# Five small loads moved behind GpSimd's first sums, and two small VectorE instructions moved later, in a two-layer graph attention kernel

## The chip, the cores and the metric

The kernel runs on one core of a Trainium2 chip. The metric is device microseconds (us) of one execution; of the kernel before there are three timed runs, and lower is better. The engines are TensorE (PE, with its weight loads as PEld), VectorE (DVE), ScalarE (ACT), GpSimd (POOL) and SyncE (SP). SP, ACT and POOL issue DMAs. All of them move their bytes on the same 16 DMA engines, through one queue for each issuer: q1 is SP's, q10 is ACT's, and q0, called software_dynamic, is GpSimd's.

## The reference

`x` is 128 graphs of 128 nodes with 512 features, float32; `adj` is one 128x128 matrix of zeros and ones that all graphs share. Two layers follow one another:

```python
# layer 0: masked attention of 8 heads, residual, layer norm
q, k, v = x @ Wq + bq, x @ Wk + bk, x @ Wv + bv
scores  = q k^T / sqrt(64) + (1 - adj) * -1e9
x = layernorm(x + softmax(scores) v @ Wo + bo)
# layer 1: additive attention, residual, layer norm
h  = x @ W
e  = leaky_relu(s1[:, :, None] + s2[:, None, :], 0.2) * adj   # s1 = h a1, s2 = h a2
x = layernorm(x + elu(softmax(e) @ h + beta * h))
```

The inputs that the change touches are `adj`, `beta` (one number), `bo` (512 numbers) and `a` (a1 and a2, 512 numbers each).

## The kernel before

**Tiling.** The 128 graphs are worked off in 64 groups of two (`G = 2`, `NG = 64`). Each big product is done with seven half-size products instead of eight (Strassen's scheme): `weight_sum` makes sums of blocks of a weight, `block_sum` makes differences of blocks of the turned x on GpSimd (n = 1, 2, 3, 4 for the tiles t1 to t4), `product` multiplies, and `take_part` and `add_block` collect the results. For the group g, `load_blocks` fetches x in blocks (tile `xblk`, one buffer, four DMAs), and `turn_x` turns it on VectorE (tile `xT`), once for each of the two graphs.

**Order.** Everything after the setup is written out by hand. `at(place, fn, ...)` puts a call on a list with a place on one common scale; the list is sorted and called in that order, which fixes the order of instructions on every engine and in every issuing queue. Groups lie `STEP = 36.678` apart, and `other` holds the places of single groups. A place is no time: an instruction runs when its engine comes to it and what it needs is there.

```python
    with tc.manual_schedule():
        for _, _, fn, args in sorted(pieces, key=lambda p: p[:2]):
            fn(*args)
```

**What lies around the change,** by engine and in the order of the places:

- SP: `load_blocks(0)` (two of its four DMAs), Wq, then Wk and Wv (`load_k_and_v`), x of graph 0 and of graph 1, `load_blocks(1)`, W (`w_sb`, place 16.793), Wo (19.493), then x and blocks of the next group.
- POOL: the setup's memsets and the identity matrix, the DMA of `adj` (L151), the four DMAs of `load_later` at 0.583 (`beta`, the two halves of `a`, `bo`; each is broadcast to all 128 partitions, L104), then `block_sum` of group 0 in the order n = 3 (7.943), 1 (11.603), 2 (12.383), 4 (16.043), `residual(0)` and `residual(1)` (L435, which add `bo` to x), the sums of Wv (L223 to L229), and `block_sum` of group 1.
- DVE: `turn_x` of group 0, the sums of Wq, `make_beta` at 12.183 (L171: identity times `beta`), the sums of Wk, `make_mask` at 16.043 (L165: (adj - 1) times 1e9), `turn_x` of group 1 (18.983 and 20.013), two `add_block` (21.043 and 21.403), then `wa_column(0, 0)` and `(0, 1)` (L180, 21.883 and 22.613, which read W and the first half of `a`), `add_block("k", 0, 4, 1, 0)` (23.343), `wa_column(0, 3)`, and the first `mask` (L387, 25.353), which reads what `make_mask` made.
- PE: `keep_busy`, 15 products of the identity with itself, the turning of the biases (L140), then the products of group 0, with the first one of group 1 (`product("k", 1, 1)`) at 21.21, and `scores(0)` (L379) at 23.903.

`beta_i`, which `make_beta` makes, is first read by `weights`, well into layer 1 of the first group. `adj_sb` itself is first read again by `edge` (L594), at 80.1 us in the trace.

Of the kernel before, what the change touches and what calls it, by code (L numbers as in the profile page):

```python
# [22 lines left out]
def gnn_two_layers(  # L23
# [34 lines left out]
    nc = tc.nc  # L58
    B, N, D = x.shape
# [10 lines left out]
    cpool = ctx.enter_context(tc.tile_pool(name="const", bufs=1))  # L70
# [31 lines left out]
    def broadcast(pool, src, n, name):  # L102
        t = pool.tile([P, n], F32, tag=name, name=f"{name}_in")
        nc.gpsimd.dma_start(out=t, in_=src.rearrange("(o n) -> o n", o=1).broadcast_to([P, n]))  # L104
        return t
# [5 lines left out]
    for i, src in enumerate((bq, bk, bv)):  # L111
        nc.scalar.dma_start(
            out=bias_rows[i * NC : (i + 1) * NC], in_=src.rearrange("(c p) -> c p", p=P)
# [34 lines left out]
    for t in s2_in:  # L148
        nc.gpsimd.memset(t, 0.0)
    adj_sb = cpool.tile([P, N], F32, tag="adj_sb", name="adj_sb")  # L150
    nc.gpsimd.dma_start(out=adj_sb, in_=adj)  # L151
    later = {}

    def load_later():
        later["beta"] = broadcast(cpool, beta, 1, "beta_b")
        for j in range(2):
            a_j = a1[j * D : (j + 1) * D].rearrange("f o -> (f o)")
            later["a", j] = broadcast(wk2, a_j, D, "uf")
        later["bo"] = broadcast(cpool, bo, D, "bo_b")


    amask = cpool.tile([P, N], F32, tag="amask", name="amask")
# [575 lines left out]
    def at(place, fn, *args):  # L738
        pieces.append((place, len(pieces), fn, args))
# [353 lines left out]
    def lay(g):  # L1093
        own = rows(g) if g < NG - 2 else last_rows(g)
        places = other.get(g, [r[0] for r in own])
        for place, (_, fn, *args) in zip(places, own):
            at(g * STEP + place, fn, *args)

    for g in range(NG):
        lay(g)  # L1100
    at(0.583, load_later)
    at(5.685, load_k_and_v)
    at(8.723, weight_sum, "q", 3, nc.vector)
    at(9.443, weight_sum, "q", 1, nc.vector)
    at(10.163, weight_sum, "q", 2, nc.vector)
    at(10.883, weight_sum, "q", 4, nc.vector)
    at(12.183, make_beta)
    at(13.163, weight_sum, "k", 3, nc.vector)
    at(13.883, weight_sum, "k", 1, nc.vector)
    at(14.603, weight_sum, "k", 2, nc.vector)  # L1110
    at(15.323, weight_sum, "k", 4, nc.vector)
    at(16.043, make_mask)
    at(16.793, load_weight, w1_sb, w1)
    at(19.323, weight_sum, "v", 3, nc.gpsimd)
    at(19.493, load_weight, wo_sb, wo)
    at(20.603, weight_sum, "v", 1, nc.gpsimd)
    at(21.883, wa_column, 0, 0)
    at(22.613, wa_column, 0, 1)
    at(23.343, weight_sum, "v", 2, nc.gpsimd)
# [55 lines left out]
```

## Time and profile before

| | us |
|---|---|
| median of 3 runs | 2377.61 |
| lowest and highest run | 2377.54, 2379.04 |
| the profiled execution: its own time | 2378.15 |
| its span (first to last instruction) | 2376.4 |
| PE busy in the span | 2354.4 (99%) |
| DVE busy | 1961.7 (83%) |
| ACT busy | 1591.1 (67%) |
| POOL busy | 865.5 (36%) |

The span is what the trace covers; 1.75 us lie around it. Times of single instructions are counted from the span's start. A line of a timeline gives start and duration in us, the engine, the line of the code, the operation, the tiles written and read, their shape, the count, and in brackets how long the engine had been idle and what ended that. The share of a DMA queue is the time of its packets over that of all 16 engines in the stretch asked for; it can go over 100% where packets overlap.

### The profile page before, as it was taken

Reading aid. Unit: us, or ns where it says so; the run is one execution under the profiler, and the core shown is the slowest. Engines: PE = TensorE matmul, PEld = TensorE weight load, DVE = VectorE, ACT = ScalarE, POOL = GpSimd, SP = SyncE. Lnnn points to the kernel's source line nnn. Section 1 sums busy time; section 2 is a strip of 40 time slices with the busy share of each in tenths; the row PEclk is TensorE's granted clock in tenths of the full one; section 3 lists DMA queues with packets and bytes.
Section 4 is the critical chain, followed back from the end, with each engine's and each line's share of the span. In section 5 each row is a group of like instructions: output and inputs, shape, how many; then the busy total and the mean of one; then the engine's idle time right before and its main releaser. Section 6 shows DMA issues by size and latency. Waiting matters only on the chain.

```text
span 2376.4 us, 50868 instructions
## 1 busy us (share of the span) xinstructions
PE 2354.4 (99%) x17703; PEld 2177.5 (92%) x17703; DVE 1961.7 (83%) x4390; ACT 1591.1 (67%) x5763; POOL 865.5 (36%) x1044
## 2 busy tenths in 40 slices
PE   8999999999999999999999999999999999999998
PEld 8998999999999999999999999999999999999996
DVE  7788788888888888888888888888888888888887
ACT  4675666766766667667666676676666766766665
POOL 6243333433433333334334333343343333433422
PEclk9999999999999999999999999999999999999999
DMA  6333334334343343343443433424434334344432
GB/s 192 108 100 112 116 101 125 107 105 134 92 120 119 107 118 108 108 128 92 121 122 103 119 108 111 126 92 121 123 103 119 107 112 125 92 120 122 116 115 74
DMA packets 256121, 269.83 MB, mean 114 GB/s; under 512 B 57372, under 2 KB 204840, under 8 KB 255480
## 3 DMA queue, kind: packets, MB, share of 16 engines
q1 hardware_dynamic: 254992, 265.45, 37.8%
q8 instruction: 140, 2.29, 0.4%
q14 instruction: 117, 0.96, 0.1%
q0 software_dynamic: 304, 0.85, 0.1%
q10 hardware_dynamic: 568, 0.27, 0.0%
HBM read 157.62 MB, written 108.85 MB: 112 GB/s over the span
## 4 chain that ended last, share of the span: by engine, by line
PE 96%; DMA 1%; DVE 1%; ACT 1%; issue 0%; SPq 0%; POOLq 0%; POOL 0%; DVEq 0%; ACTq 0%
PE pq L307 12%; PE pk L307 12%; PE pv L301 12%; PE ph L301 11%; PE pw L301 11%; PE eq L307 9%; PE psc L379 5%; PE po L454 5%; PE pz L642 5%; PE eh L301 5%; PE ew L301 4%; PE ev L301 4%; DMA xblk<-in_x_dram 1%; DMA wq_sb<-in_L_gnn_Wq_dram 0%; ACT s L401 0%
## 5 line engine op out<-in xcount | busy, mean ns | idle before, releaser
L435 POOL TENSOR_TENSOR x<-x,bo_b_in 128x512 f32<-128x512 f32 x128 | 163.6, 1279 | 863.3 <-DMA x<-in_x_dram 863.3
L401 ACT ACTIVATE s<-s,nmax 128x128 f32<-128x128 f32 x1024 | 396.9, 396 | 61.4 <-DVE nmax L395 61.3
L415 ACT ACTIVATE sb<-s,rinv 128x128 f32<-128x128 f32 x1024 | 325.3, 392 | 0.0
L355 ACT ACTIVATE kT<-pk,bias_c 128x128 f32<-128x128 f32 x512 | 160.2, 364 | 202.2 <-PE pk L307 143.2
L355 ACT ACTIVATE qT<-pq,bias_c 128x128 f32<-128x128 f32 x512 | 160.6, 368 | 157.6 <-PE pq L307 157.6
L505 DVE SCALAR_TENSOR_TENSOR ya<-w,wa_row 128x512 f32<-128x512 f32 x256 | 223.9, 875 | 4.4
L401 ACT ACTIVATION_READ_ACCUMULATOR s<-s,nmax 128x1 f32 x1024 | 199.2, 195 | 0.0
L466 ACT ACTIVATE oT<-po,bias_c 128x128 f32<-128x128 f32 x512 | 139.5, 382 | 80.5 <-PE po L454 80.5
L352 DVE TENSOR_TENSOR w<-pw,x 128x256 f32<-128x256 f32 x252 | 106.3, 422 | 97.3 <-PE pw L301 90.8
L444 DVE STREAM_TRANSPOSE attnT<-ab 128x512 f32<-128x512 f32 x256 | 172.7, 694 | 6.8 <-DMA ab<-scr 6.6
L387 DVE SCALAR_TENSOR_TENSOR s<-psc,amask 128x512 f32<-128x512 f32 x256 | 168.6, 680 | 0.7 <-PE psc L379 0.7
L395 DVE TENSOR_REDUCE nmax<-s 128x8 f32<-128x1024 f32 x128 | 156.1, 1220 | 4.3
L349 ACT COPY h<-ph 128x256 f32<-128x256 f32 x252 | 93.8, 372 | 94.1 <-PE ph L301 94.0
L349 ACT COPY v<-pv 128x256 f32<-128x256 f32 x256 | 94.6, 369 | 84.4 <-PE pv L301 59.9
L240 DVE STREAM_TRANSPOSE xT<-xblk 128x512 f32<-128x512 f32 x128 | 139.4, 1108 | 7.9 <-DMA xblk<-in_x_dram 7.9
L657 DVE SCALAR_TENSOR_TENSOR u<-h,x 128x512 f32<-128x512 f32 x126 | 87.1, 692 | 63.8 <-ACT h L349 61.6
L260 POOL TENSOR_TENSOR tx<-xT 128x256 f32<-128x256 f32 x128 | 94.7, 741 | 119.8 <-PE psc L379 97.1
L301 PE MATMUL pv<-wv_sb,xT 128*128 128x256 f32 x512 | 137.5, 392 | 0.0
L307 PE MATMUL pq<-xT,wq_sb 128*128 128x128 f32 x1024 | 135.9, 276 | 1.2 <-DMA wq_sb<-in_L_gnn_Wq_dram 1.2
L307 PE MATMUL pk<-xT,wk_sb 128*128 128x128 f32 x1024 | 134.8, 275 | 0.6 <-DMA wk_sb<-in_L_gnn_Wk_dram 0.4
L307 PEld LDWEIGHTS pq<-xT,wq_sb 128*128 128x128 f32 x1024 | 130.1, 193 | 4.5 <-issue 1.3
L307 PEld LDWEIGHTS pk<-xT,wk_sb 128*128 128x128 f32 x1024 | 129.1, 192 | 4.2 <-DMA wk_sb<-in_L_gnn_Wk_dram 0.6
(677 smaller groups left out, 6352.6 us busy)
## 6 DMA issues: line engine op xcount, KB each, us to landing
scr<-sb SPq DMA_DIRECT2D x128, 512.0 KB
ab<-scr SPq DMA_DIRECT2D x512, 128.0 KB
x<-in_x_dram SPq DMA_DIRECT2D x128, 256.0 KB
xblk<-in_x_dram SPq DMA_DIRECT2D x254, 128.0 KB
out_dram<-u SPq DMA_DIRECT2D x126, 256.0 KB
pb<-s2d SPq DMA_DIRECT2D x62, 128.0 KB
attd<-att SPq DMA_DIRECT2D x62, 128.0 KB
ab<-attd SPq DMA_DIRECT2D x248, 32.0 KB
```

Source lines behind the costliest of these rows:

```text
L301: nc.tensor.matmul(out, b[:, c, :], a[:, c, :], start=first and c == 0, stop=(c == 1), skip_group_check=True,)
L307: nc.tensor.matmul(out[:, m * N : (m + 1) * N], a[:, c, m * P : (m + 1) * P], b[:, c, :], start=first and m == 0 and c == 0, stop=(c == 1) ...
L349: nc.scalar.copy(dst, src)
L355: nc.scalar.activation(dst[:, m, :], src[:, m * N : (m + 1) * N], AF.Identity, bias=BIAS[name][:, 2 * i + m : 2 * i + m + 1],)
L387: nc.vector.scalar_tensor_tensor(s_t[b][:, j * HP : (j + 1) * HP, :], psc[b][j], SCALE, amask.rearrange("p (o n) -> p o n", o=1).broadcast ...
L395: nc.vector.tensor_reduce(nmax[b], s_t[b], AX.X, ALU.max, negate=True)
L401: nc.scalar.activation(s_t[b][:, h, :], s_t[b][:, h, :], AF.Exp, bias=nmax[b][:, h : h + 1], accum_out=rsum[b][:, h : h + 1],)
L415: nc.scalar.mul(sb[b][:, :, h, :], s_t[b][:, h, :].rearrange("p (b c) -> p b c", c=Q), rinv[b][:, h : h + 1],)
L435: nc.gpsimd.tensor_tensor(xr[b], xr[b], later["bo"], ALU.add)
L444: nc.vector.transpose(attnT[b].rearrange("p h (a r) -> p a h r", r=Q)[:, rows], ab[b].rearrange("p a (h c) -> p a h c", c=Q)[:, rows],)
L466: nc.scalar.activation(oT[b][:, c, :], src[:, c, :], AF.Identity, bias=bv_c[:, c : c + 1])
L505: nc.vector.scalar_tensor_tensor(z, y[b], 1.0, wa_row[j], ALU.mult, ALU.mult, accum_out=s12[g][:, i, j : j + 1])
```

## The change

The DMA of `adj` leaves the setup and becomes the first of `load_later`. `load_later` now issues `adj`, `beta`, `bo` and the two halves of `a`, in this order; before, `a` came ahead of `bo`. It moves from the place 0.583 to 12.183, which on POOL lies behind `block_sum` n = 3 and n = 1 of group 0 and ahead of n = 2. `make_beta` moves from 12.183 to 21.873 and `make_mask` from 16.043 to 21.878, which on DVE is behind `turn_x` of group 1 and the two `add_block` after it, and right ahead of `wa_column(0, 0)`. No instruction is added or removed.

```diff
-    nc.gpsimd.dma_start(out=adj_sb, in_=adj)
     later = {}
 
     def load_later():
+        nc.gpsimd.dma_start(out=adj_sb, in_=adj)
         later["beta"] = broadcast(cpool, beta, 1, "beta_b")
+        later["bo"] = broadcast(cpool, bo, D, "bo_b")
         for j in range(2):
             a_j = a1[j * D : (j + 1) * D].rearrange("f o -> (f o)")
             later["a", j] = broadcast(wk2, a_j, D, "uf")
-        later["bo"] = broadcast(cpool, bo, D, "bo_b")
...
-    at(0.583, load_later)
     at(5.685, load_k_and_v)
...
-    at(12.183, make_beta)
+    at(12.183, load_later)
...
-    at(16.043, make_mask)
...
+    at(21.873, make_beta)
+    at(21.878, make_mask)
     at(21.883, wa_column, 0, 0)
```

## Prediction

> **What bounds the kernel now.** I read the page's busy times and its chain of waits first, then the chain in order of time for the first 80 us, then the timeline of the engines there, and last the DMA queues in short windows.
>
> From the page, the PE row and the chain by engine:
>
> ```profile
> PE 2354.4 (99%) x17703; PEld 2177.5 (92%) x17703; DVE 1961.7 (83%) x4390; ACT 1591.1 (67%) x5763; POOL 865.5 (36%) x1044
> ...
> PE 96%; DMA 1%; DVE 1%; ACT 1%; issue 0%; SPq 0%; POOLq 0%; POOL 0%; DVEq 0%; ACTq 0%
> ```
>
> TensorE bounds it: only 2376.4 - 2354.4 = 22 us of the span are without a matmul. All that the change touches runs in the first 30 us, once. So it can move the end only by what it adds to or takes from PE's idle time at the start; afterwards PE is full and carries a shift to the end.
>
> The chain of the start, in order of time (start, duration, what):
>
> ```profile
> 1.66 8.48 DMA wq_sb<-in_L_gnn_Wq_dram
> 10.14 0.02 issue
> 10.16 0.33 SPq L81
> 10.49 0.04 issue
> 10.53 0.46 SPq L81
> 10.99 0.04 issue
> 11.04 12.89 DMA xblk<-in_x_dram
> ...
> 25.09 1.08 DVE xT L240
> 26.17 0.30 DVE kT L365
> 26.47 0.34 DVE qT L365
> 26.81 0.04 issue
> 26.86 1.16 PE eq L307 x8
> ```
>
> The start is a DMA chain. Wq lands at 10.14; SP's third and fourth issue of the next group's blocks follow it; the last block lands at 23.93; VectorE turns the blocks until 26.17, adds two results, and only then does PE's product at 26.86 go. PE waited 0.28 us at 25.21 for the turned x and 0.48 us at 26.86. **The landing of xblk of group 1 is what counts,** not the earlier landings by themselves.
>
> What stands right behind that on VectorE, and what waits for it, from the timelines of DVE and of PE's weight loads:
>
> ```profile
> 26.72 1.30 DVE L180 SCALAR_TENSOR_TENSOR wa_t<-w_sb,uf_in 128x512 f32<-128x512 f32 x1
> 28.06 1.09 DVE L180 SCALAR_TENSOR_TENSOR wa_t<-w_sb,uf_in 128x512 f32<-128x512 f32 x1
> 29.08 0.41 DVE L365 TENSOR_TENSOR kT<-eq,kT 128x256 f32<-128x256 f32 x1
> 29.55 1.42 PEld L379 LDWEIGHTS psc<-kT,qT 64*128 64x128 f32 x24 [0.19 <-DVE kT L365]
> ```
>
> VectorE has no gap from 24.05 to 30.3, and PE's scores wait 0.19 us for its add at 29.08. There is no slack between the two.
>
> The two instructions that move, in the same timeline:
>
> ```profile
> 15.21 0.28 DVE L171 TENSOR_SCALAR beta_i<-ident,beta_b_in 128x128 f32<-128x128 f32 x1
> 18.18 0.22 DVE L165 TENSOR_SCALAR amask<-adj_sb 128x128 f32<-128x128 f32 x1
> ```
>
> Now they lie beside idle time of VectorE: it idles 1.56 us ahead of 19.96.
>
> The queues from 8 to 10 us (packets, MB, share of 16 engines):
>
> ```profile
> q0 software_dynamic: 172, 0.57, 76.9%
> q1 hardware_dynamic: 34, 0.19, 23.1%
> ```
>
> GpSimd's loads hold the DMA engines just while the tail of Wq is due.
>
> **What the Trainium skill says.** "SBUF — State Buffer", section "Who interferes with whom": a VectorE `tensor_scalar` can enter a mode with two ports, and one with two SBUF inputs uses the second read port; each then contends with GpSimd, and the later one blocks until the other is through. The trace agrees: the L180 instruction takes 0.68 to 0.69 us with GpSimd idle (from 39.85 on) but 1.30 and 1.09 us beside its sums at 26.20 and 27.43; the 128x512 `tensor_scalar` of L200 takes 0.49 us at 38.79 and 0.98 us at 45.31, beside a sum. "DMA: Bandwidth & Descriptors", section "Anatomy of one DMA — SWDGE (gpsimd) path": about 2.0 us fixed plus bytes/436e3, so an estimate of 2.6 us for 256 KB. Here it is far more: adj (64 KB) landed 4.6 us after its issue, beta 6.1, the two halves of a 7.7 and 8.7, bo 10.8; I use these. The same page, section "Queues, rings and completion order": each engine takes turns between the queues it has work for. The 77 to 23 above is then no fair fight, but a sign that on most engines Wk's packets were not ready before Wq was done (Wk was issued at 6.45).
>
> **The change, part by part.** 1. *Setup on POOL.* adj's issue of 0.71 us at 1.37 goes, so the identity is ready 0.71 us earlier and `keep_busy` ends near 7.4 instead of 8.1. Worth 0: the bias turn waits for the bias DMA until 8.84 and the first real product for Wq. PE idles a little longer before it, and its clock, 0.50 from 11 to 13 us, stays as low: 0.
>
> 2. *Wq.* From 7 to 8 us q1 moved 0.24 MB; 0.19 MB was left for the time after 8. At 0.24 MB/us without q0 this is 0.8 us, so the packets end near 8.8 instead of about 9.6 (landing 10.14 less half a microsecond of receipt, my reading). PE's first product, SP's two issues behind it, and Wk start 0.8 us sooner.
>
> 3. *GpSimd's traffic comes back later.* Its share was 9.8% of 0 to 5, 34.0% of 5 to 10 and 11.7% of 10 to 15 us: 0.49 + 1.70 + 0.59 = 2.8 us of all 16 engines. After the change its issues follow the sum that ends at 8.92: adj 0.71, beta 0.57, then three of 0.55, through 11.85. With the old latencies they land from 13.5 to about 22, in a stretch where q1 alone already fills 90% (10 to 16) and 110% (16 to 24) of the engines, ahead of the xblk landing. So of the 0.77 x 2 = 1.5 us that q0 used from 8 to 10, 0.8 is won by Wk starting sooner and 0.7 is DMA time that now stands empty and is missing later. **xblk lands 0.7 us later.** Bounds: 1.8 us earlier, if the big loads slip behind xblk (0.8, and the 9.8% of 10 to 16 us, 0.6, with some 0.4 of earlier share); 2.8 later, if all the traffic returns with no win. Wk lands earlier (15.0 now), and PE gets through group 0 sooner, but this ends in a longer wait at 25.21: 0.
>
> 4. *POOL's own queue.* 2.93 us of issues stand ahead of `block_sum` n = 2 and 4, which end at 13.5 instead of 10.5. Their first reader is the product at 16.90: even 1.5 us sooner it has them. Behind stands `residual(0)`, which waited for x until 19.68 and now also needs bo, issued at 10.2: 21.0 with 10.8 us. That would hold POOL 1.3 us. Its sums of Wv and of group 1 have slack: t2, ended at 29.74, is read at 33.78, so 4.0 us. Worth 0 up to a bo landing of 23.7.
>
> 5. *SP's queue.* No issue of SP moves in order. Its W load waits for Wk (the waits view), but stands behind the fourth xblk issue, held until 14.55. 0 by itself.
>
> 6. *Beta and mask on DVE.* What leaves 15.21 and 18.18 was in idle time or ahead of sums that PE reads later: 0 gained. At the new place 0.28 + 0.22 = 0.5 us are put between the adds and `wa_column(0, 0)`; queued behind are two of these, the add at 29.08, PE's scores, and then the first mask and the row maximum. All of it shifts, and PE with it. GpSimd is in its sums there, so a wait for the port comes on top: nothing, if it only takes over the 0.6 us that the 1.30 us instruction already pays, up to twice a sum of 1.27 us less that, 1.9. I take 0.1: **0.6 us**, bounds 0.4 and 2.4.
>
> 7. *a for `wa_column`.* a's first half is issued at 10.75 and lands by 18.5 to 21.6 (7.7 to 10.8); needed at 27.2 plus the shift. 0.
>
> Sum: 0.7 + 0.6 = +1.3 us on 2378.15 for the profiled execution, 2379.45; that one stood 0.54 above the median, so 2378.9 as a median.
>
> **The rivals.** *A: the big loads slip behind xblk.* For it: round-robin, and five loads served one after another. Against it: they are on the way from 11 us on. xblk 1.8 earlier, DVE 0.6: -1.2, so 2376.4. *B, slower: the first `wa_column` waits for a.* a is now fourth in q0 and shares the engines with the 512 B pieces of xblk. From a landing at 28.0 on, each microsecond is one of VectorE, and through the add at 29.08 one of PE. Twice the 8.7 us gives 28.2, hardly anything; to cost more than 0.2% it must land near 31.5, 21 us after its issue. Then 2378.9 + 4 = 2383 or more. For it: a latency here grew from 4.6 to 10.8 us within five loads. Against it: the engines never took 20 us. *C: only VectorE's part counts,* since overlapping packets absorb q0: +0.6, 2378.2. That the change is without effect on the order is excluded: the order is by hand.
>
> **How the numbers follow.** The main case and C, which join, have 0.64; A 0.20; B 0.16, of which 0.12 over the bound. 0.2% of 2377.6 is 4.75 us, about what a measurement can tell from no change. No case gains that much: 0.02, out of A's, for what I don't see. Slower by more: 0.12. Within: 0.86. The range goes from A's 2376.2 to 2382.0, the upper bounds of parts 3 and 6 together not quite added; some 0.12 lies above and 0.06 below.
>
> **What would show it.** Right: POOL's five issues between 8.9 and 12; Wq landing near 9.3; Wk before 14.5; q0's share from 8 to 10 near 0; `turn_x` of group 1 at 24.7; beta and mask at 27.4 and 27.7, ahead of L180; a longer PE wait than 0.28 us ahead of `product("k", 1, 1)`; PE's scores 1 to 2 us later. Wrong: `turn_x` before 23.5 (A); DVE idle at L180 with the DMA of a as releaser (B); GpSimd idle for bo past 24; or a difference that arises after 50 us, which nothing here accounts for.

## The result, and the profile after

The changed kernel took **2381.16 us** in the median of 22 runs (2378.8 to 2384.34), the kernel before 2377.63 (2376.19 to 2379.73, 22 runs). The ratio, an estimate from all runs, is 1.0013, with a 95% interval of 1.0007 to 1.0018. The medians lie 3.5 us apart, where 1.3 us were forecast with a range up to 2382.0. This lies within 0.2%, the bound used for the chances, but it is clear of zero, and the forecast lies below the interval (1.7 to 4.3 us).

The profiled execution of the changed kernel took 2379.32 us, 1.8 below the median of its kernel, with a span of 2377.6, only 1.2 us above the profiled span of before. This matters below. The trace shows where 1.2 us come from; it can't show the rest.

The page after: the PE row, and the chain by engine.

```profile
PE 2353.6 (99%) x17703; PEld 2176.6 (92%) x17703; DVE 1962.0 (83%) x4390; ACT 1591.7 (67%) x5763; POOL 866.3 (36%) x1044
...
PE 94%; DMA 2%; DVE 2%; ACT 1%; SPq 1%; issue 0%; POOLq 0%; POOL 0%; ACTq 0%; DVEq 0%
```

PE does the same work. The chain has left PE for DMA and VectorE for a longer stretch, and that stretch is the start. The chain in order of time (start, duration, what):

```profile
10.21 13.89 DMA xblk<-in_x_dram
...
25.25 1.06 DVE xT L240
26.30 0.31 DVE kT L365
26.61 0.04 DVE qT L365
26.65 0.21 issue
26.86 0.50 DVE beta_i L171
27.36 0.69 DVE amask L165
28.05 0.62 DVE wa_t L180 x2
28.69 1.10 DVE wa_t L180 x2
29.79 0.34 DVE kT L365
30.13 1.34 DVE wa_t L180 x2
31.47 1.21 DVE s L387 x2
```

Three things are to be seen. The last block lands at 24.1, as late as before (23.93), although SP issued it 0.8 us sooner. The two instructions that moved, `beta_i` and `amask`, are now links of the chain, 0.50 and 0.69 us long. And PE does not appear in it before 48.56: before, its product at 26.86 was the next link.

The timeline of the changed kernel around PE's wait, with PE and then DVE:

```profile
8.67 1.13 PE L307 MATMUL pq<-xT,wq_sb 128*128 128x128 f32 x8
25.37 2.08 PE L307 MATMUL pk<-xT,wk_sb 128*128 128x128 f32 x8 [3.81 <-DVE xT L240]
27.25 1.56 PE L307 MATMUL eq<-tx,wk_sb 128*128 128x128 f32 x8
...
26.86 0.50 DVE L171 TENSOR_SCALAR beta_i<-ident,beta_b_in 128x128 f32<-128x128 f32 x1
27.28 0.77 DVE L165 TENSOR_SCALAR amask<-adj_sb 128x128 f32<-128x128 f32 x1
27.97 0.68 DVE L180 SCALAR_TENSOR_TENSOR wa_t<-w_sb,uf_in 128x512 f32<-128x512 f32 x1
```

PE starts 1.6 us sooner (8.67 against 10.28) and, in this trace, at full clock. It gets through group 0 and then waits 3.81 us, where it had waited 0.28. After this wait eight matmuls take 2.08 us instead of 1.16: the clock has fallen. The windows of the changed kernel say so (busy us of PE, PEld, DVE, ACT, POOL; then PE's clock, the share of the DMA engines, GB/s):

```profile
24.00:25.00 1.00, 0.00 (x0) 0.00 (x0) 0.77 (x1) 0.00 (x0) 0.92 (x2) 0.94 1.06 391
25.00:26.00 1.00, 0.63 (x3) 0.63 (x4) 1.00 (x2) 0.00 (x0) 0.93 (x1) 0.50 1.05 385
26.00:27.00 1.00, 1.00 (x6) 1.00 (x6) 1.00 (x4) 0.00 (x0) 0.99 (x1) 0.50 1.04 381
```

The first exponential of the first softmax starts at 33.96, against 32.88 before: 1.08 us late. At 60 us the lag is 0.9, and at the end 1.2. In between it wanders, from 0.3 to 2.0 us if one takes every row maximum after 60 us, but it doesn't grow. So all that this trace holds is settled in the first 34 us.

The queues, changed kernel, 8 to 10 us and then 10 to 15 us (packets, MB, share of 16 engines):

```profile
q1 hardware_dynamic: 79, 0.63, 79.8%
```

```profile
q1 hardware_dynamic: 278, 1.53, 76.0%
q0 software_dynamic: 52, 0.08, 5.9%
```

GpSimd's traffic has left the first stretch, as it should. But SP's queue does not take the freed time: from 10 to 15 us it moved 1.53 MB, where before it moved 1.86 MB beside 0.17 MB of GpSimd's. The engines stood partly empty, while SP's issue for W was held from 11.80 for 4.12 us. The last of the experiments comes back to this.

### The profile page after: what moved, and what is told of

It is laid out like the page before. It is cut to its first block, busy times and chain, and to the rows that moved or that the text cites. A ratio compares the mean times of both kernels' runs of the same rounds, so it can differ in the third digit from the quotient of the medians.

```text
span 2377.6 us, 50868 instructions
## 1 busy us (share of the span) xinstructions
PE 2353.6 (99%) x17703; PEld 2176.6 (92%) x17703; DVE 1962.0 (83%) x4390; ACT 1591.7 (67%) x5763; POOL 866.3 (36%) x1044
## 4 chain that ended last, share of the span: by engine, by line
PE 94%; DMA 2%; DVE 2%; ACT 1%; SPq 1%; issue 0%; POOLq 0%; POOL 0%; ACTq 0%; DVEq 0%
PE pq L307 11%; PE pv L301 11%; PE pk L307 11%; PE ph L301 11%; PE pw L301 11%; PE eq L307 9%; PE psc L379 5%; PE po L454 5%; PE pz L642 5%; PE ew L301 4%; PE eh L301 4%; PE ev L301 4%; DMA xblk<-in_x_dram 1%; ACT s L401 0%; ACT sb L415 0%
## 5 line engine op out<-in xcount | busy, mean ns | idle before, releaser
L349 ACT COPY v<-pv 128x256 f32<-128x256 f32 x256 | 94.6, 369 | 84.0 <-PE pv L301 59.6
L260 POOL TENSOR_TENSOR tx<-xT 128x256 f32<-128x256 f32 x128 | 94.6, 740 | 126.1 <-PE psc L379 98.6
```

The source lines that it names most:

```text
L349: nc.scalar.copy(dst, src)
```

## The experiments

All ratios are against the runs of the kernel before on the same chip, with 95% intervals. "Turned at" is the start of `turn_x` of group 1. It comes right after the blocks land, except in `blocks_before`, `blocks_after` and `loads_behind`, where VectorE came to it late and did not wait for them. "Lag" is that of the first exponential behind the profiled execution of before (32.88 us). Both are from one profiled execution of each kernel, while the ratio is from all runs.

| kernel | ratio | interval | turned at | lag | profiled / median us |
|---|---|---|---|---|---|
| before | | | 24.05 | 0 | 2378.15 / 2377.63 |
| changed | 1.0013 | 1.0007 to 1.0018 | 24.23 | 1.08 | 2379.32 / 2381.16 |
| after_again | 1.0013 | 1.0007 to 1.0020 | 23.24 | 0.50 | 2379.07 / 2381.72 |
| late_dve | 1.0001 | 0.9993 to 1.0009 | 24.01 | 1.55 | 2380.00 / 2378.21 |
| late_big | 1.0002 | 0.9993 to 1.0010 | 24.67 | 1.65 | 2379.48 / 2378.72 |
| after_free | 1.0012 | 1.0005 to 1.0018 | 24.12 | 0.87 | 2379.47 / 2381.40 |
| adj_early | 1.0008 | 1.0002 to 1.0015 | 26.39 | 3.42 | 2381.48 / 2380.46 |
| beta_early | 1.0010 | 1.0002 to 1.0018 | 24.61 | 2.23 | 2379.28 / 2380.37 |
| ident_late | 1.0011 | 1.0004 to 1.0018 | 25.06 | 2.07 | 2380.63 / 2380.72 |
| after_warm | 1.0024 | 1.0014 to 1.0034 | 26.95 | 4.48 | 2383.75 / 2383.75 |
| no_big | 1.0001 | 0.9993 to 1.0010 | 20.37 | -2.47 | 2375.96 / 2379.34 |
| blocks_before | 1.0007 | 0.9999 to 1.0016 | 24.93 | 1.93 | 2381.76 / 2380.72 |
| blocks_after | 1.0004 | 0.9996 to 1.0012 | 21.22 | -3.11 | 2377.61 / 2379.43 |
| loads_behind | 1.0016 | 1.0009 to 1.0022 | 24.08 | 0.59 | 2380.71 / 2382.15 |

### The changed kernel again

> The changed kernel once more, unaltered: its first profile ended 1.2 us after that of before, while its median lay 3.5 us above, so another execution is wanted. Theory S (all is settled by the landing of the blocks of group 1, by VectorE's two late instructions and by the clock that PE loses in its longer wait, within the first 50 us): the lag of this execution behind the kernel before at 50 us equals its lag at the end within 0.5 us, and the blocks land later than 24.1 us if the run is longer than 2379.3. Theory L (something later in the span): the lag at 50 us stays near 0.9 us and the rest arises after it. Time 2380 to 2383.

The ratio came back, and the profiled execution (2379.07) was the lowest of its kernel's 21 runs. It shows the same parts in other sizes: the blocks landed 1 us sooner than in the first, the clock fell later, and the end is only 0.9 us behind.

```profile
24.39 1.16 PE L307 MATMUL pk<-xT,wk_sb 128*128 128x128 f32 x8 [1.15 <-DVE xT L240]
25.88 0.28 DVE L171 TENSOR_SCALAR beta_i<-ident,beta_b_in 128x128 f32<-128x128 f32 x1
26.02 1.95 PE L307 MATMUL eq<-tx,wk_sb 128*128 128x128 f32 x8 [0.48 <-DVE qT L365]
26.86 1.11 DVE L180 SCALAR_TENSOR_TENSOR wa_t<-w_sb,uf_in 128x512 f32<-128x512 f32 x1 [0.56 <-DMA w_sb<-in_L_gnn_W_dram]
30.81 1.29 DVE L387 SCALAR_TENSOR_TENSOR s<-psc,amask 128x512 f32<-128x512 f32 x2 [0.55 <-PE psc L379]
```

Here VectorE waited 0.56 us for W, and its first mask 0.55 us for PE, which was at half clock. Blocks that land sooner are not a gain in full: W and the clock come next. What lies between this execution and the median of its kernel, 2.7 us, is not in it, so the two theories stay undecided for that part; for what it holds, the lag of 0.4 us at 51 us and 0.9 at the end agree within 0.5.

### VectorE's two instructions alone

```diff
-    at(12.183, make_beta)
-    at(16.043, make_mask)
+    at(21.873, make_beta)
+    at(21.878, make_mask)
```

> The kernel before with make_beta and make_mask alone moved to 21.873 and 21.878; the loads stay early. Theory S with the VectorE part as the main term: +1.1 us (0.50 + 0.77 us were these two beside GpSimd in the changed kernel, against 0.5 us without it), less the 0.2 us by which they had delayed the sums of Wk, so +0.5 to +1.3. The prediction's own term: +0.6. Rival theory (the loads cost, VectorE's part is hidden): 0 within the interval.

The trace shows a larger price than expected, the runs none. In the profiled execution both instructions took far longer than before, beside GpSimd's sums of Wv at 26.50 and of x at 27.72:

```profile
26.69 1.15 DVE L171 TENSOR_SCALAR beta_i<-ident,beta_b_in 128x128 f32<-128x128 f32 x1
27.77 0.76 DVE L165 TENSOR_SCALAR amask<-adj_sb 128x128 f32<-128x128 f32 x1
30.66 1.61 PE L379 MATMUL psc<-kT,qT 64*128 64x128 f32 x24 [1.14 <-DVE kT L365]
```

1.15 + 0.76 us instead of 0.28 + 0.22, and PE's scores wait 1.14 us for the add behind them. But over the runs the ratio is 1.0001; this execution (2380.0) was next to the slowest of 13 (2377.14 to 2380.03). So VectorE's part, though it is plainly in the chain, is too small to be told from nothing: up to 0.0009, 2.1 us.

### The big loads alone

```diff
-    at(0.583, load_later)
+    at(0.583, load_beta)
...
+    at(12.184, load_later)
```

`load_later` holds only bo and a here, and adj stays in the setup.

> The kernel before with only bo and a (768 KB of the 832 KB) moved behind the first sums; adj and beta stay early, and make_beta and make_mask stay at 12.183 and 16.043. Theory S: Wq lands sooner than 10.14 (near 9.0), the blocks of group 1 near 24 us as in the other two, PE waits over 3 us ahead of its product at 25.2 and runs at half clock after it: about +1.0 us from the clock, or +2.5 if the landing is often later than in the one profile. Rival (VectorE's part is the whole cost): 0 within the interval. Rival of a gain (earlier Wq moves everything): 1 us or more faster.

Wq's first product starts at 9.80, the blocks are turned at 24.67, and PE waits 2.2 us. The clock is at half from 26.8 on. The lag of 1.65 us fits the first theory, but again the runs differ by nothing that can be told: 1.0002. A gain of 1 us is not excluded (0.9993 is 1.7 us); a loss as large as that of the changed kernel is (1.0010 is 2.4 us).

### The changed kernel with beta and mask out of the chain

```diff
+    at(18.973, make_beta)
+    at(18.978, make_mask)
...
-    at(21.873, make_beta)
-    at(21.878, make_mask)
```

> The changed kernel with make_beta and make_mask ahead of turn_x of group 1 (18.973 and 18.978), where VectorE stood idle for 5.6 us; adj and beta have landed by then (14.4 and 15.9 us). Theory S: 1.1 us faster than the changed kernel, because the two instructions leave the chain, so +2.4 on the median of before if the whole median shift of 3.5 is real. Rival (VectorE's part is hidden anyway): as slow as the changed kernel.

The chain of this trace has neither instruction in it, yet the time stays: 1.0012 against 1.0013, where 1.1 us would be 0.0005. The intervals are too wide to exclude the full 1.1 us. But even the lower bound of this kernel, 1.0005, leaves 1.2 us of loss without VectorE's part.

### Which early piece is missed

Three kernels put one piece back. `adj_early` issues adj in the setup again. `beta_early` issues beta at 0.583. `ident_late` leaves all loads late and delays the identity:

```diff
+    pad = cpool.tile([P, 768], F32, tag="pad", name="pad")
+    nc.gpsimd.memset(pad, 0.0)
     make_identity(nc, ident)
```

> The changed kernel with the DMA of adj back in the setup; beta, bo and a stay late, and make_beta and make_mask stay at 21.873 and 21.878. The moved loads bo and a alone came out 0.5 us above the kernel before, make_beta and make_mask alone 0.0, the whole change 3.5. Theory I (the identity is ready 0.7 us sooner, PE warms up too early and then stands idle): the identity is late again here, so near the kernel before, +0 to +1 us. Theory F (GpSimd's very first DMA is dear when nothing small goes ahead of the loads that are waited for): also +0 to +1 us. Theory T (all five loads together late are too many for the stretch): beta is 0.5 KB, so the 64 KB of adj would have to be it, and a third or less is won back.

> The changed kernel with the DMA of beta alone (0.5 KB) issued in the setup's place; adj, bo and a stay late. Theory F: near the kernel before, +0 to +1 us, since a DMA of GpSimd has gone ahead. Theory I: the identity is late again by this issue of 0.57 us, so it too expects a gain; together with the next kernel the two part. Theory T: as slow as the changed kernel, +3 to +3.5.

> The changed kernel with one memset of 128x768 on GpSimd ahead of the identity (about 0.7 us), so that PE's warm-up starts as late as before (2.5 us); all five loads stay late. Theory I: near the kernel before, +0 to +1 us. Theories F and T: as slow as the changed kernel, +3 to +3.5.

All three came out between 1.0008 and 1.0011, below the changed kernel and above the expectation of theories I and F (up to 1 us, 1.0004); the intervals of all three reach down to 1.0004 or below it, and overlap that of the changed kernel. So none of the three pieces is seen to carry the loss alone, and none is cleared either. In two of the traces the blocks land late, and these are worth a look. In `adj_early`:

```profile
22.50 1.06 PE L307 MATMUL pk<-xT,s_k 128*128 128x128 f32 x8
26.39 2.09 DVE L240 STREAM_TRANSPOSE xT<-xblk 128x512 f32<-128x512 f32 x2 [5.75 <-DMA xblk<-in_x_dram]
27.54 1.16 PE L307 MATMUL pk<-xT,wk_sb 128*128 128x128 f32 x8 [3.98 <-DVE xT L240]
29.18 2.08 PE L307 MATMUL eq<-tx,wk_sb 128*128 128x128 f32 x8 [0.48 <-DVE qT L365]
33.71 1.29 DVE L387 SCALAR_TENSOR_TENSOR s<-psc,amask 128x512 f32<-128x512 f32 x2 [0.30 <-PE psc L379]
```

The blocks land 2.3 us later than before, PE waits 3.98 us and then runs at half clock, and the first exponential is 3.42 us late; the span ends 3.3 us late. In the trace's packets the pieces of 512 B, which are the blocks, thin out over three microseconds: 82 of them start from 22 to 23 us, then 62, 38 and 3, while 112 to 145 packets of 2 KB, the next loads, go in each of these microseconds. It looks as if a few of the 16 engines were still at the blocks when the others had gone on; the trace does not name the engine of a packet. **The landing is that of the last piece.**

### Keeping PE's clock up

```diff
+    at(21.2, keep_busy, 11, "warm")
```

> The changed kernel with 11 products of the identity with itself (22 matmul records) on PE at place 21.2, ahead of its wait for the turned blocks of group 1. Theory C (the longer wait lets PE's clock fall to a half, and the next 3 us cost 1 to 2 us more): 1 to 2 us faster than the changed kernel, PE's clock 1.0 from 24 to 29 us. Rival (the clock's fall is hidden by VectorE, which is the slower of the two from 26 to 31 us): no faster; more than 0.5 us slower if the added products end after the blocks land.

It settles nothing on the clock. The added products ran from 23.31 to 25.9, but in this execution the blocks landed at 26.9; PE idled 2.17 us more, and the clock was at half from 29.3 to 32.7. The lag also grows later on, from 5.1 us at 51 us to 6.4 at 269. The added PSUM tile shifts the turn of the eight buffers, which may be why; this is not shown. The ratio is 1.0024.

### Without the big loads

```diff
-        later["bo"] = broadcast(cpool, bo, D, "bo_b")
+        later["bo"] = cpool.tile([P, D], F32, tag="bo_b", name="bo_b_in")
+        nc.gpsimd.memset(later["bo"], 0.0)
...
```

The two tiles of a are filled in the same way, with 0.01.

> The changed kernel with the three big loads of GpSimd (bo and the two halves of a, 768 KB) left out: memsets of the same tiles stand in their place on GpSimd, so bo counts as 0 and a as constant. adj and beta stay late, and nothing else moves. Theory Q (GpSimd's big loads, brought into the stretch in which x and the blocks of group 1 come, make the blocks land late and unevenly): the blocks land at 22.5 us or earlier, PE waits under 2.5 us for them, and the time is 3 to 5 us below the changed kernel, below the kernel before by 0 to 1.5. Rival (the blocks are late by SP's own queue, whose issues run ahead sooner): the blocks at 24 to 26 us as in the changed kernel, and its time within 1 us.

Without the 768 KB the ratio is 1.0001 against 1.0013; the intervals overlap from 1.0007 to 1.0010. Its trace is what was expected:

```profile
20.37 2.13 DVE L241 STREAM_TRANSPOSE xT<-xblk 128x512 f32<-128x512 f32 x2 [1.87 <-DMA xblk<-in_x_dram]
23.05 1.22 DVE L172 TENSOR_SCALAR beta_i<-ident,beta_b_in 128x128 f32<-128x128 f32 x1
27.09 1.61 PE L380 MATMUL psc<-kT,qT 64*128 64x128 f32 x24 [1.20 <-DVE kT L366]
```

The blocks are turned 3.7 us sooner than before, and the next wait is VectorE's part. But only three of its 13 runs (2375.59, 2375.96, 2376.16) are as fast as this; the others lie from 2378.2 to 2381.31. So most executions lose 2 us or more somewhere even without the big loads. That they lose it in the start is likely, but there is no trace of one.

### The blocks ahead in SP's queue

```diff
         load_turned(wk_sb, wk)
+    def load_v():
+        fetch_blocks(1)
         load_turned(wv_sb, wv)
+        fetch_x(0)
```

`load_v` stands at 6.723. `blocks_before` has this on the kernel before, `blocks_after` on `after_free`, with three `wa_column` moved as well. x of graph 0 is at 6.483 in the order and stays ahead of the blocks.

> The kernel before with SP's loads in another order: the blocks of group 1 go ahead of Wv and of x of graph 1 (1.25 MB), instead of behind them; all else as before. If the landing of these blocks is the end of the start's chain, they now land near 19 to 21 us, PE's product for group 1 no longer waits for them, and the gain is what PE waited there, 0.3 and 0.5 us, so 0.5 to 1 us faster. If Wk's landing or VectorE decide instead: 0. If Wv is now late for PE at 31 us: slower by what it waits.

> The changed kernel with make_beta and make_mask ahead of turn_x of group 1, with the blocks of group 1 ahead of Wv and x of graph 1 in SP's queue, and with the first three wa_column behind the first row maxima on VectorE (26.7, 26.8 and 29.0), since W lands no sooner. If the late landing of the blocks is what costs the change its time, the early landing of Wk (11.6 to 13.5 us against 15.1) now reaches PE: blocks at 18 to 21 us, no wait of PE over 1 us after 12 us, 1 to 3 us faster than the kernel before, 4 to 6 below the changed kernel. If a late landing of W or of Wv takes its place: between the two.

On the kernel before it didn't help. Wk, which lies ahead of the blocks, landed later:

```profile
16.63 3.53 PE L311 MATMUL pk<-xT,wk_sb 128*128 128x128 f32 x16 [2.72 <-DMA wk_sb<-in_L_gnn_Wk_dram]
24.93 2.13 DVE L244 STREAM_TRANSPOSE xT<-xblk 128x512 f32<-128x512 f32 x2
```

PE waited 2.72 us for Wk, at half clock after it, and VectorE turned the blocks without any wait for them, behind PE's products of group 0. On the changed kernel the blocks were turned at 21.22, also without a wait, and the first exponential came 3.11 us sooner than before; but the lag is +0.53 by 41 us. The moved `wa_column` stood ahead of the softmax's reciprocal, and PE waited 1.31 us for GpSimd's differences, which stood behind Wv's sums:

```profile
32.15 1.16 PE L311 MATMUL pq<-tx,s_q 128*128 128x128 f32 x8 [1.31 <-POOL tx L264]
35.74 1.63 DVE L180 SCALAR_TENSOR_TENSOR wa_t<-w_sb,uf_in 128x512 f32<-128x512 f32 x1
```

With 1.0004 it is no faster than before, and nearer to it than the changed kernel is.

### The big loads behind everything

```diff
-    at(0.583, load_later)
+    at(0.583, load_beta)
...
+    at(19.333, load_later)
...
-    at(21.883, wa_column, 0, 0)
+    at(29.0, wa_column, 0, 0)
```

> The kernel before with adj, beta, make_beta and make_mask as they were, but bo and a issued only behind GpSimd's first sum of Wv (19.333), which waits for Wv, so that they come after the blocks of group 1; residual(0) and (1) move behind them to 33.8 and 33.9, and the first three wa_column behind the row maxima (29.0 to 29.2), so that nobody waits for bo and a. Theory Q (the big loads of GpSimd in one stretch with x and the blocks are what makes the blocks late and uneven): the blocks are turned at 20 to 22 us, and the kernel is 1.5 to 3 us faster than before, the runs as close together as those of before. Rival (the lateness of the blocks comes from SP's own row of loads; without the big loads one profile was fast, but most runs were not): turned at 23 us or later, and no faster than before by more than 1 us.

The time of turning looks like a failure of theory Q, but it is not one. GpSimd issued the big loads at 18.7, and SP's queue had the engines to itself from 10 to 16 us (95.6%, and no GpSimd packet). The blocks did land sooner: no 512 B piece of them starts after 21 us, where before 19 start from 22 to 23 us. But VectorE came late to them, and turned them at 24.08 without a wait. With `residual` moved away, GpSimd began its sums of Wv at 17.28 instead of 22.14, beside VectorE's last sums of Wk and the mask:

```profile
17.68 1.64 DVE L229 TENSOR_TENSOR s_k<-wk_sb 128x512 f32<-128x512 f32 x1
19.35 1.65 DVE L231 TENSOR_TENSOR s_k<-wk_sb,s_k 128x512 f32<-128x512 f32 x1
20.92 1.28 DVE L167 TENSOR_SCALAR amask<-adj_sb 128x128 f32<-128x128 f32 x1
```

Before, these three took 0.69, 0.69 and 0.22 us. So the kernel doesn't decide on theory Q. In its trace most of the lag comes from something else that it brought along, five `wa_column` in a row ahead of the reciprocal (L410).

```profile
39.86 0.69 DVE L182 SCALAR_TENSOR_TENSOR wa_t<-w_sb,uf_in 128x512 f32<-128x512 f32 x1
40.48 0.20 DVE L410 RECIPROCAL rinv<-rsum 128x8 f32<-128x8 f32 x1
40.71 2.45 ACT L417 ACTIVATE sb<-s,rinv 128x128 f32<-128x128 f32 x8 [3.02 <-DVE rinv L410]
```

ScalarE waits 3.02 us, and the lag goes from 0.59 to 3.71. None of the versions beats the kernel before.

**The empty engines.** Read side by side, the traces say more about the fifth of the engines' time that stood empty. It is not spread over the stretch from 10 to 15 us. The table has the busy share of the 16 engines and what they moved from 14 to 15 us, then how much of the engines' time SP's and GpSimd's queues used from 13 to 17 us.

| kernel | loads of GpSimd that are late | share | GB/s | SP | GpSimd |
|---|---|---|---|---|---|
| before | none | 0.98 | 414 | 99.0% | 1.3% |
| loads_behind | bo and a, after 23 us | 0.97 | 401 | 102.9% | 0 |
| late_big | bo and a | 0.89 | 219 | 38.6% | 52.5% |
| no_big | adj and beta | 0.28 | 72 | 70.4% | 4.8% |
| changed | all five | 0.25 | 60 | 33.4% | 35.1% |
| after_again | all five | 0.14 | 25 | 31.7% | 30.6% |

SP's blocks were issued by then and had not landed, so there was work. Yet in the changed kernel SP's queue lost 66% of the engines' time while GpSimd's used 35%: these loads cost SP's queue about twice their own engine time. The small ones, which move next to nothing, do it too. In `beta_early`, with only beta's 0.5 KB on GpSimd's queue, SP's queue used 35.0% of the engines from 4 to 6 us; in the five traces with all five loads late, which have no GpSimd packet there, it used 79.5 to 94.6%. These are single traces, and no kernel left adj or beta out, so the reason stays open.

## Why the prediction was right, and where it was off

The direction, the place and the bound were right: the change acts in the first 34 us, it costs a little, and nothing of it goes on afterwards. The sum was too small, +1.3 us against +3.5. That the first profiled execution, 2379.32, so nearly meets the 2379.45 forecast for it is luck: its blocks came 0.18 us later and VectorE's part cost 1.07; in the second the blocks came 0.81 sooner, W and the clock took that back, and the end was at +0.9. Step by step:

- **Step 1, the identity.** It was ready 1.06 us sooner (PE starts at 1.48 instead of 2.54). "The clock stays as low" held in one trace and not in the other: the first eight products took 2.05 us before, 1.13 in the first trace of the changed kernel and 2.05 in the second. It stayed worth 0, for the reason given in step 3: a longer wait at the blocks.
- **Step 2, Wq.** Right in direction, short in size: VectorE's first sum of Wq starts at 8.55 instead of 10.17, 1.6 us against 0.8. The reason given, the big loads' traffic from 8 to 10 us, does not hold by itself. In the seven traces with some GpSimd load in the setup's place the first product starts at 9.80 to 11.05, among them `loads_behind`, which had only adj and beta there (11.05), and `beta_early`, with 0.5 KB (10.76). In the seven without, it starts at 8.67 to 9.87.
- **Step 3, the blocks.** Predicted 0.7 later, with bounds of -1.8 and +2.8. In the two traces of the changed kernel it measured +0.18 and -0.81; over the eight traces in which bo and a are issued there, with SP's order as it was, the turning starts at 23.24 to 26.95, with a mean of 24.91, which is +0.86. So the mean came near the number, but executions differ by more than the whole term, and a fixed number was the wrong form for it. The budget of engine time behind it failed in both halves. The head start was larger: by 13 us SP's queue had moved 3.26 MB instead of 2.39, an estimated 2.3 us at the 1.86 MB that it moved from 10 to 15 us before, where 0.8 us were counted. And GpSimd's loads did not just take their own engine time: from 13 to 17 us SP's queue used 33.4% of the engines instead of 99.0% while GpSimd's used 35.1%, and by 17 us it was behind (3.72 against 3.91 MB).
- **The clock after PE's wait** was in no step. PE idle at the blocks was put at 0. The wait itself is free, but in seven of those eight traces the clock is at half for the 3.4 us after it (`beta_early`, where PE waited 1.06 us, is the exception; the last section says what decides). In the second trace of the changed kernel this and not VectorE holds the first mask (0.55 us).
- **Steps 4 and 5, POOL's and SP's order.** Right, but for the 0.56 us that VectorE waited for W in the second trace. bo landed 8.0 us after its issue, `residual(0)` started at 18.36, sooner than before (19.68), and nobody waited for GpSimd's sums.
- **Step 6, beta and mask.** 0.6 predicted, bounds 0.4 and 2.4; 27.97 - 26.72 - 0.18 = 1.07 us in the first trace, 1.8 in `late_dve`. GpSimd was at its sums both times, which fits the reason that was named, its port; in the second trace the two took 0.28 and 0.23 us, as if alone. Over the runs it can't be seen, and so rival C, that this part alone counts, is not borne out: taken away (`after_free`) it leaves 1.0012.
- **Step 7, a.** Landed by 21.5, needed at 27.97: rival B did not occur. Rival A, the big loads slipping behind the blocks, did not either. The second trace shows its sign, turning before 23.5 us, but not its mechanism: from 20 to 21 us 348 pieces of the blocks start and no packet of GpSimd's.

What stays open is about 2 us. The two profiled executions of the changed kernel lie 1.8 and 2.7 us below the medians, and no trace of a longer one was had. That the longer ones have their blocks at 25 to 27 us, as in `adj_early`, `ident_late` and `after_warm`, would fit: the lags there are 2.1 to 4.5 us. But that is argued from sister kernels. What the runs suggest is that the big loads in this stretch are needed for the loss (1.0013 with them, 1.0001 without, in intervals that just overlap), and that alone they don't make it (`late_big`, 1.0002). Which of the small pieces it takes beside them, the runs can't tell. Why the last pieces of the blocks trail by up to three microseconds, and why SP's queue stands still beside GpSimd's loads, wasn't found.

## What to carry to other kernels

A start that ends with one landing is not helped by landings that come sooner ahead of it: PE gained 1.6 us, spent them in a wait that grew from 0.28 to 3.81 us, and came out of the wait at half clock. Free engine time in a DMA budget is not time that the next load will take; look at whether the queue really fills it, and at what it moves while another issuer's loads are on the way. And when a change is worth a thousandth, compare the profiled execution with its own kernel's runs before reading a size from it: here the two profiles of the changed kernel would have told 1 us where the runs tell 3.5.

## What the hardware showed that was not expected

- PE's clock falls for 3.4 us at a time, and a wait much shorter than that can lower it. In `after_again` PE waited 1.15 and 0.48 us between 23 and 26.1, and the clock was at half from 26.2 to 29.6; before, with 0.28 and 0.48 us, it stayed at full. The Trainium skill, "TensorE: Matmul & The Clock Gate", section "Part 1: The HAM clock gate (the "warmup" mystery)", speaks of at least one idle window of about 3.4 us; here less was enough.
- What decides is how much PE works in a fixed cell of time. In each of the 14 traces all changes of the clock lie on one grid of 3.413 us, which starts at another point in each. The first 60 us of the traces hold twelve stretches at half clock, all one cell long. Eleven follow a cell in which PE was busy for 1.60 us or less, and no such cell is followed by full clock there. Every cell with 1.80 us or more is followed by full clock; from 1.73 to 1.78 us one is followed by half and five by full. So the limit is near half a cell, and the same wait lowers the clock or not by where the grid cuts it, which differs from execution to execution:

| trace | cell, us | PE busy, us | clock in the next cell |
|---|---|---|---|
| before | 6.74 to 10.15 | 1.60 | 0.50 |
| changed | 4.41 to 7.82 | 2.07 | 1.00 |
| changed | 21.47 to 24.88 | 0.10 | 0.50 |
| after_again | 5.71 to 9.12 | 1.59 | 0.50 |
| after_again | 22.78 to 26.19 | 1.78 | 0.50 |
| beta_early | 24.11 to 27.52 | 1.87 | 1.00 |
| adj_early | 21.82 to 25.24 | 1.74 | 1.00 |

- One broadcast of 0.5 KB from GpSimd at the start went with a Wq landing as late as with all 832 KB: first product at 10.76 with beta alone there, 10.28 with all, 8.67 and 9.16 with none (the two traces of the changed kernel).
- The first loads differ from execution to execution by about as much as the change is worth: the same program had its blocks of group 1 turned at 24.23 in one execution and 23.24 in another, and small edits with SP's order unchanged gave anything up to 26.95.
